# Two layers planned in one list, the second layer's first chunk prepared within the first layer

## Chip, cores and metric

The kernel runs on one core of a Trainium2 chip. The metric is the device time of one execution in microseconds. A core has five engines with queues of their own, each worked through in order: PE (matrix products and transposes), DVE (vector work and the scans), ACT (activations and copies), POOL (elementwise work) and SP, which here issues the DMAs. Engines wait for one another by semaphores. Work that waits at the head of a queue holds everything behind it.

## What is computed

A network of two layers over two batches of 2048 rows of 256 values, all in float32. Each layer is a state-space block followed by a feed-forward part. Layer 0 has a scan over 256 channels with 16 states and an expert part that sends each row through chosen small networks; layer 1 is a bidirectional Mamba (a forward and a backward pass over each batch, 512 channels, 16 states) with a small feed-forward network, and a second feed-forward whose weights go through a butterfly transform. Cut to what matters:

```python
def _selective_scan(u, dt, A, Bm, Cm, Dp):
    h0 = jnp.zeros((u.shape[0], D_INNER, D_STATE), u.dtype)
    def step(h, inp):
        u_t, dt_t, B_t, C_t = inp
        dA = jnp.exp(dt_t[:, :, None] * A)
        h = dA * h + (dt_t * u_t)[:, :, None] * B_t[:, None, :]
        y = jnp.einsum('bds,bs->bd', h, C_t)
        return (h, y)
    ...

def _mamba(x, Win, convw, convb, Wx, Wdt, bdt, Alog, Dp, Wout):
    xz = x @ Win
    xi, z = jnp.split(xz, 2, axis=-1)
    xi = jax.nn.silu(_causal_dwconv(xi, convw, convb))
    xdbc = xi @ Wx
    ...
    dt = jax.nn.softplus(dt_in @ Wdt + bdt)
    A = -jnp.exp(Alog)
    y = _selective_scan(xi, dt, A, Bm, Cm, Dp)
    return y * jax.nn.silu(z) @ Wout
```

Layer 1 normalises the sum that layer 0 leaves (x1, kept in DRAM as x1d, one tensor for each batch) and feeds it to `_mamba`.

## The kernel before

**A planner sets the order.** Every piece of work is an `op`: an engine, an estimated duration, a Python function that emits the instructions, a key (when it is due), the ops it depends on, and the rings of buffers that it takes (`takes`). `Plan.order` walks the ops as a list scheduler: on each engine it picks, among those that could start at once, the one with the smallest key; an op that takes a buffer may not run further ahead of the oldest unfinished scan than `ahead` key units. The order it returns is the order on PE, DVE, ACT and POOL. DMAs on SP are placed by the framework. `spread` gives a group of ops keys in a given interval.

**Layer 0** (`layer0`) has 8 chunks of 512 rows, 4 for each batch, 32 key units each. A chunk has 16 pairs of scans. A pair goes through ACT (two decays, L1140), PE (two sources, L1164), DVE (two scans, L1172), POOL (the last column kept, L1187, and the product with cb, L1191), PE (the collecting matmul, L1195). Its cb and G come by DMA (L1148, L1152) into rings of three. Beside the scans run: the prologues of both batches; `prepare` of the next chunk; the experts, eight groups `experts(b, ec)` due one every 27 key units from key 12 (L664 to L840: gather, first and second matmul, store to interd, relay, back-projection, added to xacc); two butterflies (`butterfly_ops`) which make the weights wup and wdn for layer 1 and store them. The end of a chunk is `finish` (the output matmul L1226, added to xacc at L1233); when all ten sums of a quarter of a batch are in, xacc is stored to x1d (L651).

**Layer 1** (`layer1`) has 16 chunks of 512 rows (forward and backward, two batches), 64 key units each, 64 scans each (L1935, with sources L1922, decays L1904, products L1954, collecting L1966, fills of the source rows on ACT L1846 and POOL L1848). Before a chunk's scans comes its preparation. For the first chunk this is `prologue(0, 0)`: two halves of 256 rows, each loaded from x1d (L1401), moments (L1375, L1376), the root on POOL (L59, L60), normalised (L81), turned on PE (L1414), copied (L1421); the second half is loaded only when the first is copied. Then `prepare(0)`: the projection (L1606), a copy (L1613), the halo (L1618 to L1621), the convolution's taps on DVE (L1631), SiLU (L1689), the projection to dt, B and C (L1700, L1706, L1730, L1741, L1754), softplus (L1770), dt times u (L1784), turned and copied (L1793, L1799). In later chunks the same work runs beside the scans of the chunk before. The second prologue, `prologue(0, 1)`, and the loads of layer 1's weights (`load_in`, `load_z`, `load_out`, `load_ff`) are due before or at the start of the first chunk. `load_ff` loads eight small rows (L1516 to L1529), wup, wdn and two feed-forward weights (L1545 to L1555), and sums the bias rows on POOL (L1537 to L1540).

**Between the layers** stands a wall. Each layer has a plan of its own, and each opens its memory pools and its eight PSUM banks on entry and closes them on leaving. Layer 1's pools take the place of layer 0's, and its list begins when layer 0's has been emitted in full:

```python
    layer0(tc, c, a, x1d, wupd, wdnd, bupd)
    layer1(tc, c, a, x1d, wupd, wdnd, bupd, out)
```

Of the kernel before, what the change touches and what calls it, by code (L numbers as in the profile page):

```python
# [10 lines left out]
F32 = mybir.dt.float32  # L11
# [8 lines left out]
B = 2  # L20
# [79 lines left out]
EARLY0, GATE0, PREP0, FIN0, PRO0, EXP0, BFLY0 = -2, (10, 15), (8,30), (4, 12), ((-1, 8), (4, 14)), (12, 27), ((8, 110), (114, 200))  # L100

SLACK = 0.15

# [251 lines left out]
def layer0(tc, c, a, x1d, wupd, wdnd, bupd):  # L355
    nc = c.nc
    with ExitStack() as ctx:
        c.banks(ctx, sums=4, work=2)
        wp = ctx.enter_context(tc.tile_pool(name="w0", bufs=1))
        fp = ctx.enter_context(tc.tile_pool(name="ffn0", bufs=1))  # L360
        ap = ctx.enter_context(tc.tile_pool(name="attn0", bufs=1))
        sp = ctx.enter_context(tc.tile_pool(name="scan0", bufs=1))
        bf = ctx.enter_context(tc.tile_pool(name="bfly", bufs=1))

        xnd = [c.dram.tile([L, D], F32, name=f"xnd{b}") for b in range(B)]
        xnTd = [c.dram.tile([P, 2, L], F32, name=f"xnTd0{b}") for b in range(B)]
        interd = [
            [c.dram.tile([P, 16, D], F32, name=f"interd{b}{ec}") for ec in range(4)] for b in range(B)
        ]


        rings = {
            "pp": 2, "ab": 2, "yacc": 4, "xp": 1, "lt": 1, "xq": 2, "selT": 1, "pb": 2, "PT": 4,
            "f1": 1, "f2": 1, "inner": 1, "stage": 2, "relay": 2, "xacc": 4, "xnT": 3, "zs": 1,
            "cv": 2, "uw": 1, "par": 1, "dt": 3, "dw": 3, "lk": 1, "a": RING0, "cb": CB0, "G": 3,
            "bfy": 1, "bft": 1, "bf8": 2,
        }
        pl = Plan(rings, AHEAD0)
        op, inline = pl.op, pl.inline

        def rows4(ref, q):

            return ref.rearrange("(n p) d -> p n d", p=P)[:, 4 * q : 4 * q + 4, :]

        W, M = {}, {}
# [3 lines left out]
        def weights():  # L389
            def first():  # L390
                W["cw"] = wp.tile([P, 2, 4], F32, name="cw")
                nc.sync.dma_start(W["cw"], a["conv0"].rearrange("(k p) c -> p k c", p=P))
                W["wpar"] = wp.tile([P, 2, 112], F32, name="wpar")
                nc.sync.dma_start(W["wpar"], a["wpT"].rearrange("(k p) e -> p k e", p=P))
                W["wdt"] = wp.tile([64, 512], F32, name="wdt")
                nc.sync.dma_start(W["wdt"], a["wdtT"])
                W["bdt"] = wp.tile([P, 4], F32, name="bdt")
                nc.sync.dma_start(W["bdt"], a["dt0"])

            def scans():  # L400
                W["A"] = wp.tile([P, 4, NS], F32, name="A")
                nc.sync.dma_start(W["A"], a["A0"])
                W["As"] = wp.tile([P, 4, 8], F32, name="As")
                nc.sync.dma_start(W["As"], a["A0s"])
                W["D0"] = wp.tile([64, 4], F32, name="D0")
                nc.sync.dma_start(W["D0"], a["D0"])

            def other():
                W["ctrl"] = wp.tile([P, 2, 64], F32, name="ctrl")
                nc.sync.dma_start(W["ctrl"], a["ctrl"].rearrange("(k p) e -> p k e", p=P))  # L410
                W["wz"] = wp.tile([P, 2, D], F32, name="wz")
                nc.sync.dma_start(W["wz"], a["wzT"].rearrange("(k p) e -> p k e", p=P))
                W["wo"] = wp.tile([P, 2, D], F32, name="wo")
                nc.sync.dma_start(W["wo"], a["woT"].rearrange("(k p) d -> p k d", p=P))
                W["fbias"] = wp.tile([P, 32], F32, name="fbias")
                nc.sync.dma_start(W["fbias"], a["fbias"])

            def exps():
                nc.scalar.activation(W["As"], W["As"], AF.Exp)
                nc.scalar.activation(W["A"], W["A"], AF.Exp)  # L420

            def factors():
                A = W["A"]
                nc.vector.tensor_scalar(W["As"], W["As"], -1.0, None, ALU.mult)

                small = wp.tile([P, 4, NS], F32, name="small")
                nc.vector.tensor_scalar(small, A, 1e-5, None, ALU.is_lt)
                large = wp.tile([P, 4, NS], F32, name="large")
                nc.vector.tensor_scalar(large, small, -1.0, 1.0, ALU.mult, ALU.add)
                c1 = wp.tile([P, 4, NS], F32, name="c1")  # L430
                nc.vector.tensor_scalar(c1, A, -1.0, 1e-10, ALU.mult, ALU.add)
                nc.vector.tensor_mul(c1, c1, large)
                nc.vector.tensor_sub(c1, c1, small)
                nc.vector.reciprocal(c1, c1)
                nc.vector.tensor_mul(c1, c1, large)

                cf = W["cf"] = wp.tile([P, 4, NS], F32, name="cf")
                nc.vector.tensor_copy(cf[0:64], c1[0:64])
                nc.vector.tensor_copy(cf[64:P], small[64:P])
                fold = W["fold"] = wp.tile([P, 64], F32, name="fold")  # L440
                nc.vector.tensor_add(fold, c.ident[:, 0:64], c.ident[:, 64:P])
                W["Gd"] = c.dram.tile([P, 4, 8, P], F32, name="Gd")

            def sources(h):

                if h == 0:
                    W["G"] = fp.tile([P, 4, NS, 64], F32, tag="selT", name="G")
                G = W["G"]
                nc.vector.tensor_mul(
                    G[:, h],  # L450
                    W["fold"].unsqueeze(1).broadcast_to([P, NS, 64]),
                    W["cf"][:, h].unsqueeze(2).broadcast_to([P, NS, 64]),
                )

            def store(h):
                nc.sync.dma_start(
                    W["Gd"][:, h].rearrange("p m e -> p (m e)"),
                    W["G"][:, h].rearrange("p n e -> p (n e)"),
                )

            def lacks():

                nc.vector.tensor_scalar(W["cf"][0:64], W["cf"][0:64], -1.0, None, ALU.mult)

            def turn():
                W["ps"] = c.pp()
                for h in range(4):
                    nc.tensor.transpose(
                        W["ps"][0:16, h * P : (h + 1) * P], W["cf"][:, h], c.ident
                    )  # L470

            def turned():
                W["cl"] = wp.tile([112, 2, P], F32, name="cl")
                v = W["ps"][0:16].rearrange("p (e h c) -> p e h c", h=2, c=P)
                for h in range(2):
                    nc.vector.tensor_copy(W["cl"][64 + 32 * h : 80 + 32 * h], v[:, :, h])

            def masks():
                tie_i = W["tie_i"] = wp.tile([64, 16], I32, name="tie_i")
                nc.gpsimd.iota(tie_i, pattern=[[1, 16]], base=0, channel_multiplier=0)  # L480

                block = W["block"] = wp.tile([P, 8, 16], F32, name="block")
                nc.gpsimd.memset(block, 1.0)
                nc.gpsimd.affine_select(
                    out=block, in_=block, compare_op=ALU.is_ge, fill=0.0, base=0,
                    pattern=[[-16, 8], [0, 16]], channel_multiplier=1,
                )
                nc.gpsimd.affine_select(
                    out=block, in_=block, compare_op=ALU.is_ge, fill=0.0, base=15,
                    pattern=[[16, 8], [0, 16]], channel_multiplier=-1,  # L490
                )

            def ties():
                tie = W["tie"] = wp.tile([64, 16], F32, name="tie")
                nc.vector.tensor_copy(tie, W["tie_i"])
                nc.vector.tensor_scalar(tie, tie, 1e-6 / 15.0, None, ALU.mult)

            M["first"] = op(SP, 0.3, first, key=-40)
            s = M["scans"] = op(SP, 0.3, scans, key=-39)
            M["w"] = op(SP, 0.4, other, key=-36)  # L500
            e = op(ACT, 0.45, exps, s, key=-39, table="exp")
            f = op(DVE, 2.0, factors, e, key=-38)
            M["As"] = f
            M["G"] = []
            for h in range(4):
# [3 lines left out]
                if h == 0:  # L509
                    g0 = g  # L510
# [8 lines left out]

        def prologue(b, q, k0, k1, keep=None):
            S = {}
            n0 = len(pl.ops)

# [1917 lines left out]
```

## Time and profile before

| | us |
|---|---|
| median of 3 executions | 2895.32 (2892.51 to 2903.18) |
| the profiled execution, whole | 2900.49 |
| its span, first to last instruction | 2898.4 |
| busy PE, DVE, ACT, POOL | 2634.8 (91%), 2366.5 (82%), 2153.3 (74%), 2246.7 (78%) |
| layer 0: first scan starts, last scan ends | 51.5, 884.0 |
| layer 0's chunks 0 to 7, first scan to last | 97.6, 107.5, 113.7, 114.7, 102.3, 95.1, 112.8, 79.5 |
| layer 1: first scan starts, last scan ends | 966.6, 2838.5 |
| layer 1's chunks 0 to 3 | 100.5, 112.7, 110.9, 111.5 |

A profile is of one execution, so lengths within it belong to 2898.4, not to the median. The busy share of PE is modelled: its matmuls overlap. A line such as L1172 is the line of the program that made the instruction. The chain of work that ended last has PE for 38% of the span, DVE for 14% and POOL for 10%; its heaviest single lines (PE L1922 10%, PE L1966 8%, DVE L1935 7%, POOL L1954 7%) are layer 1's scans and their neighbours.

### The profile page before, as it was taken

Reading aid. Unit: us, or ns where it says so; the run is one execution under the profiler, and the core shown is the slowest. Engines: PE = TensorE matmul, PEld = TensorE weight load, DVE = VectorE, ACT = ScalarE, POOL = GpSimd, SP = SyncE. Lnnn points to the kernel's source line nnn. Section 1 sums busy time; section 2 is a strip of 40 time slices with the busy share of each in tenths; the row PEclk is TensorE's granted clock in tenths of the full one; section 3 lists DMA queues with packets and bytes.
Section 4 is the critical chain, followed back from the end, with each engine's and each line's share of the span. In section 5 each row is a group of like instructions: output and inputs, shape, how many; then the busy total and the mean of one; then the engine's idle time right before and its main releaser. Section 6 shows DMA issues by size and latency. Waiting matters only on the chain.

```text
span 2898.4 us, 43538 instructions
## 1 busy us (share of the span) xinstructions
PE 2634.8 (91%) x15268; PEld 1878.3 (65%) x15268; DVE 2366.5 (82%) x2508; ACT 2153.3 (74%) x3301; POOL 2246.7 (78%) x2149
## 2 busy tenths in 40 slices
PE   6888998999994899999999899999999999999997
PEld 2334543444442577777777777778787788787875
DVE  5967776676664689989889999898898988989894
ACT  4645755657641998988988888788889898887871
POOL 2867447754442699989899999898998998988894
PEclk7999999999997999999999999999999999999998
DMA  6576467755554121321131222222212212121211
GB/s 222 171 211 186 142 186 226 244 167 171 161 159 159 51 82 46 98 71 59 56 97 47 88 85 67 91 81 70 70 52 82 63 59 84 55 67 56 66 59 55
DMA packets 256203, 308.92 MB, mean 107 GB/s; under 512 B 25264, under 2 KB 190256, under 8 KB 254064
## 3 DMA queue, kind: packets, MB, share of 16 engines
q1 hardware_dynamic: 255984, 306.13, 34.0%
q8 instruction: 121, 1.98, 0.3%
q14 instruction: 98, 0.80, 0.1%
HBM read 246.55 MB, written 59.51 MB: 106 GB/s over the span
## 4 chain that ended last, share of the span: by engine, by line
PE 38%; DVE 14%; POOL 10%; issue 4%; ACT 2%; DMA 1%; SPq 0%; POOLq 0%; DVEq 0%; ACTq 0%
PE ab L1922 10%; PE yacc L1966 8%; DVE a L1935 7%; POOL a L1954 7%; PE pp L2150 3%; PE pp L2036 3%; PE pp L1606 3%; PE pp L2107 2%; PE pp L1577 2%; PE pp L2218 2%; POOL bT L1848 2%; DVE xn L81 2%; DVE pp L1631 1%; PE pp L1700 1%; PE pp L2246 1%
## 5 line engine op out<-in xcount | busy, mean ns | idle before, releaser
L1954 POOL TENSOR_TENSOR a<-a,cb 128x1024 f32<-128x1024 f32 x512 | 1216.7, 2376 | 29.7 <-POOL hc L1948 0.2
L1935 DVE TENSOR_TENSOR_SCAN a<-a,hc,ab 128x512 f32<-128x512 f32 x768 | 943.5, 1266 | 84.2 <-PE ab L1922 63.5
L1904 ACT ACTIVATE a<-dt,A 128x512 f32<-128x512 f32 x1024 | 677.4, 716 | 46.4 <-PE yacc L1966 30.3
L1922 PE MATMUL ab<-ident,bT 128*128 128x128 f32 x4096 | 626.5, 277 | 56.8 <-DVE a L1935 48.5
L1922 PEld LDWEIGHTS ab<-ident,bT 128*128 128x128 f32 x4096 | 486.7, 142 | 240.3 <-DVE a L1935 138.5
L1966 PE MATMUL yacc<-ident,a 128*128 128x128 f32 x4096 | 562.5, 275 | 22.3 <-POOL a L1954 22.1
L1966 PEld LDWEIGHTS yacc<-ident,a 128*128 128x128 f32 x4096 | 470.9, 141 | 63.5 <-POOL a L1954 35.2
L1846 ACT ACTIVATE bT<-dtuT,BT 128x512 f32<-128x512 f32 x640 | 423.8, 714 | 26.5 <-PE ab L1922 26.5
L1935 DVE TENSOR_TENSOR_SCAN a<-a,ab 128x512 f32<-128x512 f32 x256 | 299.4, 1206 | 37.0 <-PE ab L1922 30.3
L1172 DVE TENSOR_TENSOR_SCAN a<-ab,hn,a 128x512 f32<-128x512 f32 x192 | 242.2, 1275 | 102.8 <-PE ab L1164 97.9
L1191 POOL TENSOR_TENSOR a<-a,cb 128x1024 f32<-128x1024 f32 x128 | 307.6, 2403 | 10.4 <-POOL hn L1187 0.3
L1187 POOL COPY hn<-a 128x2 f32<-128x2 f32 x128 | 50.2, 393 | 322.5 <-DVE a L1172 302.9
L1164 PE MATMUL ab<-dw,Gm 128*128 128x512 f32 x512 | 275.9, 636 | 15.0 <-DVE a L1172 8.4
L1848 POOL TENSOR_SCALAR bT<-dtuT,BT 128x512 f32<-128x512 f32 x384 | 273.3, 716 | 8.0 <-ACT dtuT L1799 3.3
L1140 ACT ACTIVATE a<-dt,As 128x512 f32<-128x512 f32 x256 | 173.4, 715 | 132.5 <-PE yacc L1195 61.2
L1164 PEld LDWEIGHTS ab<-dw,Gm 128*128 128x128 f32 x512 | 85.5, 194 | 136.0 <-issue 65.9
L1948 POOL COPY hc<-a 128x2 f32<-128x2 f32 x512 | 107.7, 210 | 82.8 <-DVE a L1935 80.1
L1195 PE MATMUL yacc<-a,fold 128*64 128x512 f32 x512 | 137.7, 616 | 8.5 <-POOL a L1191 8.5
L1606 PE MATMUL pp<-xnT,winx 128*128 128x512 f32 x256 | 128.6, 607 | 5.7 <-DVE zu L1631 4.8
L2036 PE MATMUL pp<-wout,ygT 128*128 128x256 f32 x512 | 130.7, 381 | 2.7 <-DVE zu L1631 2.5
L1577 PE MATMUL pp<-winz,xnT 128*128 128x512 f32 x256 | 126.7, 602 | 4.2 <-DVE zu L1631 4.2
L2107 PE MATMUL pp<-xnT,wup 128*128 128x256 f32 x512 | 122.9, 385 | 3.7 <-ACT gff L2116 1.0
(200 smaller groups left out, 4128.1 us busy)
## 6 DMA issues: line engine op xcount, KB each, us to landing
cb<-bcd SPq DMA_DIRECT2D x256, 256.0 KB, 3.2
cb<-cd SPq DMA_DIRECT2D x256, 128.0 KB, 3.1
Gm<-Gd SPq DMA_DIRECT2D x128, 128.0 KB, 3.2
xnq<-xnd SPq DMA_DIRECT2D x32, 512.0 KB, 5.4
f<-in_f_dram SPq DMA_DIRECT2D x32, 512.0 KB, 4.9
interd<-stage SPq DMA_DIRECT2D x64, 256.0 KB, 4.5
relay<-interd SPq DMA_DIRECT2D x64, 256.0 KB, 3.4
xnTd<-xnT SPq DMA_DIRECT2D x16, 512.0 KB, 4.2
```

The source lines that it names most:

```text
L1164: nc.tensor.matmul(R["x", h], R["G"][:, h, :], ck.dw[e][:, h, :], start=True, stop=True)
L1172: nc.vector.tensor_tensor_scan(v, R["x", h], v, 0.0 if ck.first else pv.hn[:, k, h : h + 1], ALU.add, ALU.mult,)
L1191: nc.gpsimd.tensor_mul(v, v, R["cb"].unsqueeze(1).broadcast_to([P, 2, T]))
L1606: nc.tensor.matmul(S["ps"], w["winx"][:, k, e * P : (e + 1) * P], ck.xnT[:, k, :], start=(k == 0), stop=(k == 1),)
L1846: nc.scalar.activation(t, ck.dtuT[:, q, :], AF.Copy, scale=v)
L1848: nc.gpsimd.tensor_scalar(t, ck.dtuT[:, q, :], v, 1.0, ALU.mult, ALU.mult)
L1904: nc.scalar.activation(R["a"][:, h], ck.dt[:, e0 + h], AF.Exp, scale=w["A"][:, e0 + h, n : n + 1],)
L1922: nc.tensor.transpose(R["b", h][:, q * P : (q + 1) * P], ck.bT[n, q][:, e * P : (e + 1) * P], c.ident,)
L1935: nc.vector.tensor_tensor_scan(v[:, step], v[:, step], b[:, step], 0.0 if ck.first else pv.hn[:, e, n : n + 1], ALU.mult, ALU.add,)
L1954: nc.gpsimd.tensor_mul(v, v, ck.cb[n].unsqueeze(1).broadcast_to([P, 2, T]))
L1966: nc.tensor.matmul(ck.y[e][:, tb * P : (tb + 1) * P], v[:, tb * P : (tb + 1) * P], c.ident, start=False, stop=(n == NS - 1), is_transpose= ...
L2036: nc.tensor.matmul(S["ps"][:, n * D : (n + 1) * D], ck.ygT[:, e, q * P : (q + 1) * P], ck.w["wout"][:, e, :], start=(e == 0), stop=(e == 3),)
```

## The change

Both layers become one list of ops in one `Plan`, ordered in one go, with one set of PSUM banks. Layer 1's keys are rescaled to follow layer 0's (`STEPS0 + PACE * key`, so 64 units of layer 1 are 35.2 of the plan), and its first prologue is due at -75 to -58 of its own units, which is 214.75 to 224.1 of the plan; layer 0's last chunk has the keys 224 to 256. The planner's `ahead` is layer 0's 4 for both (layer 1 had 7 in its own units, 4 is 7.3 of them).

Pools are opened and closed from within the list. They are of a class `Late` that opens a pool when told, on the left or right side of memory, with waits for reused memory set tile by tile. On the right side stand layer 0's pools of the experts and butterflies, replaced (op `sw1`) when their last op is done by layer 1's pools for the direction's weights, the preparation and the normalised rows. On the left stand layer 0's weights, preparation and scans, replaced (op `sw2`) when all of layer 0 is done by layer 1's shared weights, scans and feed-forward. Both ops emit no instruction; layer 1's ops depend on the one whose memory they use. So its preparation may run once the experts are through, its scans, fills and the loads of `load_ff` only after layer 0's end.

To free the right side sooner, the experts of batch 1 are due from key 127 at one every 20 units (from 120, every 27). xacc moves to a left pool. `finish` of the last chunk is due at 256 to 258 rather than 260 to 268, the loads of batch 1's xacc at 140 rather than 172. Rings that both layers had under one name get a name for each. The indentation of both layers changes, which makes every line of them part of the full diff; its core, without that:

```diff
+FIRST, SECOND, STEPS0, PACE = (-75, -58), (-60, 0), 256, 0.55
+class Late:
+    def __init__(self, tc, name, bufs=1, side="left"):
+        self.args = dict(name=name, bufs=bufs, side=side, reuse_waits="tile")
+        self.tc = tc
+    def open(self):
+        self.cm = self.tc.tile_pool(**self.args)
+        self.pool = self.cm.__enter__()
+    def close(self):
+        self.cm.__exit__(None, None, None)
+    def tile(self, *args, **kw):
+        return self.pool.tile(*args, **kw)
...
-            fetch_sums(b, q, (K * (NT + 1) + 8) * b + 4)
+            fetch_sums(b, q, (K * NT + 8) * b + 4)
...
-            finish(i, K * (i + 1) + FIN0[0], K * (i + 1) + FIN0[1])
+        finish(i, *((K * (i + 1) + k for k in FIN0) if i + 1 < len(steps) else (K * (i + 1), K * (i + 1) + 2)))
...
         for p in range(2 * 4):
-            at = EXP0[0] + EXP0[1] * p
-            experts(p // 4, p % 4, at, at + EXP0[1], at + 2 * EXP0[1])
+        at, n = (EXP0[0] + EXP0[1] * p, EXP0[1]) if p < 4 else (EXP1[0] + EXP1[1] * (p - 4), EXP1[1])
+        experts(p // 4, p % 4, at, at + n, at + 2 * n)
...
-            ld = op(SP, 0.1, load, *copies, takes=("xnT", "x1t") if h == 0 else ("x1t",))
+            ld = op(SP, 0.1, load, sw1, x1_stores[b, k], *copies, takes=("xnT", "x1t") if h == 0 else ("x1t",))
...
-        r = op(SP, 0.6, rows)
-        x = op(SP, 0.2, extra, takes=("xn", "xn"))
+        r = op(SP, 0.6, rows, sw2)
+        x = op(SP, 0.2, extra, sw2, takes=("xn", "xn"))
...
-        pl.spread(n0, -140, -120)
+    pl.spread(n0, *FIRST)
...
+    for o in pl.ops[start:]:
+        o.key = STEPS0 + PACE * o.key
+    return pl.ops[start:]
...
-    layer0(tc, c, a, x1d, wupd, wdnd, bupd)
-    layer1(tc, c, a, x1d, wupd, wdnd, bupd, out)
+    c.banks(ctx, sums=4, work=2)
...
+    pl = Plan(rings, AHEAD0)
+    left0 = [Late(tc, n) for n in ("w0", "attn0", "scan0")]
+    right0 = [Late(tc, n, side="right") for n in ("ffn0", "bfly")]
+    right1 = [Late(tc, n, k, "right") for n, k in (("wdir", 1), ("mamba", 2), ("row1", 1))]
+    left1 = [Late(tc, n, k) for n, k in (("w1", 1), ("scan1", 4), ("tmp1", 1))]
...
+    r, x1_stores, ops0 = layer0(tc, c, a, pl, pools, x1d, wupd, wdnd, bupd)
+    last = max(o.key for o in r)
+    sw1 = pl.op(SP, 0.0, lambda: swap(right0, right1), *r, key=last)
+    sw2 = pl.op(DVE, 0.0, lambda: swap(left0, left1), *ops0, key=STEPS0)
+    layer1(tc, c, a, pl, pools, x1d, wupd, wdnd, bupd, out, x1_stores, sw1, sw2)
+    swap([], left0 + right0)
+    with tc.manual_schedule(engines={nc.tensor.engine, nc.scalar.engine, nc.vector.engine, nc.gpsimd.engine}):
+        for o in pl.order():
+            o.f()
+    swap(left1, [])
+    swap(right1, [])
```

## Prediction

> **What bounds the kernel now.** I read first the slices of the page, to see where no engine is full. One slice is 72.5 us; the thirteenth (869 to 942 us) stands out on every engine.
>
> ```profile
> PE   6888998999994899999999899999999999999997
> DVE  5967776676664689989889999898898988989894
> ACT  4645755657641998988988888788889898887871
> POOL 2867447754442699989899999898998998988894
> PEclk7999999999997999999999999999999999999998
> ```
>
> Then busy time by stage, with stages cut at the scans (L1172 in layer 0, L1935 in layer 1): layer 0's chunks 5, 6 and 7, the stretch between the layers, layer 1's chunk 0. Columns: stretch, length, then busy us of PE, weight load, DVE, ACT, POOL, the granted clock, DMA share, GB/s.
>
> ```profile
> 595.10:690.50 95.40, 92.87 (x396) 43.47 (x394) 73.35 (x85) 66.54 (x109) 49.88 (x38) 0.98 0.52 161
> 690.50:804.60 114.10, 106.36 (x508) 57.58 (x508) 70.69 (x73) 69.20 (x108) 47.73 (x38) 1.00 0.52 164
> 804.60:884.00 79.40, 73.26 (x266) 31.16 (x264) 50.31 (x49) 27.50 (x43) 39.41 (x31) 0.98 0.48 146
> 884.00:966.60 82.60, 36.52 (x125) 20.10 (x124) 20.66 (x43) 30.16 (x45) 14.11 (x28) 0.75 0.43 140
> 966.60:1070.70 104.10, 92.95 (x626) 73.78 (x625) 92.85 (x92) 98.58 (x150) 97.74 (x100) 1.00 0.18 56
> ```
>
> Layer 0 is paced by PE (92 to 97% busy in these chunks, DVE 62 to 77%); layer 1 has PE, DVE, ACT and POOL all near 90%. Between them 82.6 us pass without a scan, and no engine is half full. The timeline there (start, us, engine, line; in brackets the idle time before and what ended it) shows one chain:
>
> ```profile
> 881.59 2.46 DVE L1172 TENSOR_TENSOR_SCAN a<-ab,hn,a 128x512 f32<-128x512 f32 x2 [0.75 <-PE ab L1164]
> 884.38 2.34 POOL L1191 TENSOR_TENSOR a<-a,cb 128x1024 f32<-128x1024 f32 x1
> 886.77 1.08 PE L1195 MATMUL yacc<-a,fold 128*64 128x512 f32 x4 [2.56 <-POOL a L1191]
> 888.66 3.29 PE L1226 MATMUL pp<-wo,zs 128*128 128x256 f32 x14 [0.19 <-DVE zs L1207]
> 893.19 0.38 SPq L651 DMA_DIRECT2D x1d<-xacc  x1
> 907.37 1.88 DVE L81 TENSOR_SCALAR xn<-x1t,mv,rs 128x256 f32<-128x256 f32 x4 [13.59 <-POOL obias L1539]
> 922.10 0.43 DVE L1375 BATCH_NORM_STATS2 bs<-x1t 128x6 f32<-128x256 f32 x1 [12.85 <-DMA x1t<-x1d]
> 942.64 1.91 ACT L1689 ACTIVATE zu<-zu 128x2048 f32<-128x2048 f32 x1
> 966.63 10.24 DVE L1935 TENSOR_TENSOR_SCAN a<-a,ab 128x512 f32<-128x512 f32 x9 [5.99 <-PE ab L1922]
> ```
>
> The last scan of layer 0 ends at 884.05, its output projection at 891.95, the last store is issued at 893.19. All after that is layer 1's first chunk made ready: two halves loaded and normalised (to 925), projection and convolution (to 942), SiLU, parameters, softplus, transposes (to 963), first scan at 966.63. None of it needs that last store: it reads batch 0, stored long before.
>
> **The change, part by part.** The built programs hold the same instructions but for one activation table load more (131 for 130; 1.28 us in this trace, on ACT, 27.5 us busy of 79.4 in chunk 7: nothing). So only places move. I counted each engine's list between scans, before and after. Up to layer 0's chunk 4 and from layer 1's chunk 2 the counts agree but for about 2 us; costs fall in four stages. For PE, whose matmuls overlap, I price an instruction by the time it adds to the union of PE's busy time.
>
> *Chunks 5 and 6: the experts of batch 1 come sooner.* Chunk 5 gains 16 back-projections (L833, 0.54), 16 gathers (0.24), 16 first (0.14) and 8 second (0.28) expert matmuls and 16 transposes (0.13), less two L1105: +17.7 us of PE. Chunk 6 loses 9.3. PE is nearly full there, nothing hides it: +8.4. Bounds: 0, since DVE has 65 us idle in the two, and 17.
>
> *Chunk 7: the preparation moves in.* PE gains 16 transposes L1414 (2.8), 8 L1606 (7.2), 4 L1700 (3.6), 4 L1730 (2.2), 4 L1754 (0.5), 16 L1793 (1.9), 18.2 us, and loses 8.4 of expert work: +9.8. DVE gains 8 L1375, 8 L1376, 12 L1631 (0.75 each), 3 L1784 and 8 L81, less three others: +22.8 us, against 29.1 idle. Beside POOL's products L81 is dear: of its 160 in the trace the 77 that overlap a product take 1397 ns on average, the other 83 take 582; at the mean of 974 that I used, eight lack 8 x 0.42 = 3.4 us. POOL gains 6.6 us (40 idle), SP some two dozen issues of 0.4 to 0.6 us among loads of cb that wait on POOL for 29.1 us of this chunk. If all hides in idle time, 0; if DVE's share is simply added, 22.8 + 3.4 = 26; PE alone at its 94% share, 9.8/0.94 = 10.4. I take 15.6, a third of the way from PE's 10.4 to DVE's 26, since PE is the fuller engine. Layer 0 grows by 8.4 + 15.6 = 24, bounds 0 and 43.
>
> The Trainium skill, SBUF — State Buffer, section "Who interferes with whom", says that a two-port DVE operation and a GpSimd one hold their shared port exclusively, the loser waiting out the whole instruction; by that rule the products could as well be held, 8 x 0.58 = 4.7 us on POOL, which has 40 idle, so 3.4 us less and 2849; but the trace shows the wait on DVE (1397 against 582 ns) and the product unmoved (2.37 us beside a scan, 2.39 beside L81), so the sum keeps the 3.4.
>
> *The gap.* In the new order PE has, after the last output matmul, 16 transposes that add the skip term (L1881, two groups of 1.04) and then the first source (4 transposes, 0.66). From the last scan: 891.95 - 884.05 + 2.1 + 0.7 = 10.7 us to the first scan of layer 1, instead of 82.6. Fills on POOL (4 of 0.7 after the last product) are ready by then. If the new pools' tiles must wait for the last store to land (893.19 + 2.92), then fills and source: 896.1 + 2.7 + 0.7 - 884.05 = 15.5. That is the upper bound; 10 the lower.
>
> *Start of layer 1.* The loads that need the old pools' memory now stand behind the last store on SP: eight small rows (0.45 each), the first cb, four weight tensors of 3.1 MB, then the next cb. First cb: 893.19 + 0.38 + 3.6, landing 3.5 us later, about 900.8; POOL's sums of the bias rows (L1537 to L1540) stand before the first product too. So the first product comes 6.0 us after the first scan (894.8), against 2.7 now (969.29). 3.1 MB at the 400 GB/s seen at 910 to 920 take 8 us, so the second cb lands near 909 for a product due at 908. I take +4; with 3.6 us net more of PE in chunks 0 and 1, mostly beside this, +5. Bounds 0 and 16: the weights took 9.0 to 10.7 us to land before. A queue of nine ring buffers lets 18 scans run on meanwhile, but POOL is 94% busy in this chunk and doesn't win the time back.
>
> Sum: -82.6 + 10.7 + 24 + 5 = -42.9. The profiled execution took 2900.5 us (span 2898.4, 2.1 around it), 5.2 over the median; 2895.3 - 42.9 = **2852 us**.
>
> **Rivals.**
> *Layer 0 absorbs it all* (chance 0.16). For: DVE, ACT and POOL are idle for 29 us and more in chunk 7, and a busy PE is only modelled. Against: PE's 97% in chunk 5. Layer 0 +3, start +3: -82.6 + 10.7 + 6 = -66, 2829 us. The Trainium skill speaks for this one (Perfetto Trace Analysis, "Identifying the Most-Contended Engine": matmul busy time misjudges PE, weight-load busy time is the measure, and that is 46 to 50% of chunks 5 and 6 here).
>
> *Layer 1 starves at its start* (0.15): cb and bias rows late behind the weights, first products stall. For: the 1.5 to 2 times longer landings in today's hole. Gap 15.5, start +14: -82.6 + 15.5 + 24 + 14 = -29, 2866 us.
>
> *It slides out* (0.07): the preparation stands in the order early but its loads come late on SP (the second half of x1t is loaded only after the first is turned), so convolution and after (927 to 967, 40 us, with 5 to get there) still follow the last scan, and layer 0 grows a little less: -82.6 + 45 + 20 + 5 = -13, 2882 us. This is where the change would not do what it says. Against: in the built order PE's and DVE's whole part of it stands ahead of layer 0's last scan.
>
> *Lock-step, slower* (0.07): the preparation is some 25 dependent steps across five in-order queues, and each holds the scans behind it for one product (2.36 us): 59 us in chunk 7, with 8.4 and 10.4 of PE 78, so -82.6 + 10.7 + 78 + 5 = +11, 2906 us. It decides once layer 0 grows by more than 67 us. For: scans in layer 0 wait for PE in 18 of 32 cases in chunk 7. Against: the planner puts scans between the steps.
>
> **How the numbers follow.** Forecast 0.55, with its own range 2838 to 2868 (the bounds of chunk 7 and the start, not all at once). About 0.5%, 14.5 us, is what a measurement of this kernel can tell from no change. Faster: 0.55 + 0.16 + 0.15 = 0.86; within: 0.07; slower: 0.07. The range goes from 2826 (all absorbed) to 2888 (slid out), leaving out lock-step and tails.
>
> **What would show it.** Chunk 5 near 113 us, chunk 6 near 105, chunk 7 near 95; first L1935 scan some 11 us after the last L1172; granted clock near 1.0 in place of 0.75 around it; first L1954 product some 6 us after that scan; chunks from layer 1's second on unchanged within 1%. It would be wrong if chunk 7 passes 130 us, if the gap stays above 40, or if later chunks change, which the equal order excludes.

## The result, and the profile after

The changed kernel takes 2871.63 us, the median of 4 executions (2868.0 to 2875.17); the kernel before, run beside it, 2899.06 (2892.51 to 2903.18). The ratio is 0.9907 with a 95% interval of 0.9881 to 0.9933: 27.4 us, where 42.9 were forecast. The time lies outside the forecast's own range (2838 to 2868) and inside the outer one (2826 to 2888). The profiled execution took 2875.17 us, its span 2873.5 (24.9 less than the 2898.4 before).

The slices of the changed kernel, 71.8 us each; the hole of the thirteenth is gone:

```profile
PE   6889988998998799999999899999999999999997
DVE  5967776677467789989989999998898988989884
ACT  4636755567457698898998888888889898887871
POOL 2867346753255899989899999898899998989894
PEclk7999998999999999999999999999999999999998
```

The timeline where the hole was (start, us, engine, line; in brackets the idle time before):

```profile
919.27 1.28 DVE L1182 TENSOR_TENSOR_SCAN a<-ab,hn,a 128x512 f32<-128x512 f32 x1
...
925.19 3.29 PE L1236 MATMUL pp<-wo,zs 128*128 128x256 f32 x14 [0.19 <-DVE zs L1217]
...
928.31 1.91 PE L1882 MATMUL yacc<-ident,a 128*128 128x128 f32 x16
...
930.06 1.04 PE L1923 MATMUL ab<-ident,bT 128*128 128x128 f32 x8
930.77 2.33 DVE L1936 TENSOR_TENSOR_SCAN a<-a,ab 128x512 f32<-128x512 f32 x2 [1.57 <-ACT a L1905]
```

The last scan of layer 0 ends at 920.55 and the first of layer 1 (L1936 now, L1935 before) starts at 930.77. What stands between is what the forecast named: the output matmuls, the 16 skip transposes, the first source. Busy time by stage, layer 0's chunks 5, 6, 7, the gap, layer 1's chunk 0 (stretch, length, busy us of PE, weight load, DVE, ACT, POOL, granted clock, DMA share, GB/s):

```profile
599.00:716.20 117.20, 109.44 (x513) 58.01 (x512) 89.88 (x97) 77.77 (x126) 52.58 (x40) 0.97 0.51 161
716.20:827.10 110.90, 102.62 (x459) 49.66 (x458) 62.27 (x62) 66.16 (x104) 44.54 (x35) 0.98 0.53 164
827.10:920.60 93.50, 85.27 (x260) 34.10 (x258) 69.70 (x86) 46.52 (x65) 46.84 (x50) 0.95 0.51 154
920.60:930.80 10.20, 8.40 (x47) 5.90 (x48) 2.10 (x4) 9.96 (x17) 5.26 (x7) 1.00 0.22 73
930.80:1056.70 125.90, 103.23 (x658) 81.50 (x657) 93.78 (x95) 96.21 (x147) 105.19 (x106) 0.92 0.27 86
```

| stage, us | before | after | difference | forecast |
|---|---|---|---|---|
| layer 0, chunks 3 and 4 | 223.1 | 227.9 | +4.8 | 0 |
| chunk 5 | 95.4 | 117.2 | +21.8 | +17.7 |
| chunk 6 | 114.1 | 110.9 | -3.2 | -9.3 |
| chunk 7 | 79.5 | 93.5 | +14.0 | +15.6 |
| between the layers | 82.6 | 10.2 | -72.4 | -71.9 |
| layer 1, chunks 0 and 1 | 216.8 | 236.1 | +19.3 | +5 |
| layer 1, chunks 2 to 15 | 1655.1 | 1645.8 | -9.3 | 0 |

The hole closed as forecast. Of its 72 us, layer 0 took 36.7 back (24 forecast; chunks 1 and 2, not in the table, changed by -0.7) and the start of layer 1 took 19.3 (5 forecast). The -9.3 at the end was in no term of the forecast. It sits mostly in chunks 7 and 14 of layer 1 (3.7 us each). A kernel whose layer 1 is the unchanged one (the first experiment) has 1650.2 there, with chunk 14 as fast as here, and the changed order ran there between 1642.8 and 1652.9 us in the profiles below; so it need not be the change's, and some of the profiled gain is chance.

The start of layer 1. First the longest waits in that chunk (who waited for whom: us in all, times, longest), then POOL's timeline, then SP's:

```profile
DVE a L1936 <- PE ab L1923: 21.4, 10, 14.6
...
PE pp L2108 <- DMA wup<-wupd: 12.2, 1, 12.2
...
POOL fwnb L1538 <- DMA fwnb<-in_fwn_b_dram: 8.6, 1, 8.6
```

```profile
923.34 2.71 POOL L1849 TENSOR_SCALAR bT<-dtuT,BT 128x512 f32<-128x512 f32 x4
934.69 0.87 POOL L1538 TENSOR_SCALAR fwnb<-fwnb 128x256 f32<-128x256 f32 x1 [8.65 <-DMA fwnb<-in_fwn_b_dram]
...
941.97 2.34 POOL L1955 TENSOR_TENSOR a<-a,cb 128x1024 f32<-128x1024 f32 x1 [0.23 <-DMA cb<-bcd]
951.47 0.19 POOL L1949 COPY hc<-a 128x2 f32<-128x2 f32 x1 [7.15 <-DVE a L1936]
```

```profile
929.23 0.37 SPq L661 DMA_DIRECT2D x1d<-xacc  x1
929.65 0.50 SPq L1517 DMA_DIRECT2D fwnw<-in_fwn_w_dram  x1
...
934.12 0.36 SPq L1837 DMA_DIRECT2D cb<-bcd  x1
934.68 2.20 SPq L1546 DMA_DIRECT2D wup<-wupd  x2
```

Two heads of queues block here. On PE the first up projection of the feed-forward (L2108) stands in line and waits 12.2 us for wup, whose loads were issued only at 934.68; every source behind it is late, so the scans wait too (one wait of 14.6 us). On POOL the sums of the bias rows (L1538 to L1541) stand ahead of the first product, which comes 11.2 us after the first scan (6.0 forecast, 2.7 before).

### The profile page after: what moved, and what is told of

Read it like the earlier page. It is cut to its first block, busy times and chain, and to the rows that moved or that the text cites. A ratio compares the mean times of both kernels' runs of the same rounds, so it can differ in the third digit from the quotient of the medians.

```text
span 2873.5 us, 43499 instructions
## 1 busy us (share of the span) xinstructions
PE 2639.9 (92%) x15268; PEld 1877.2 (65%) x15268; DVE 2378.0 (83%) x2508; ACT 2153.4 (75%) x3302; POOL 2245.8 (78%) x2149
## 4 chain that ended last, share of the span: by engine, by line
PE 53%; POOL 16%; DVE 14%; issue 7%; DMA 5%; ACT 4%; SPq 1%; POOLq 0%; DVEq 0%; ACTq 0%
PE ab L1923 10%; POOL a L1955 8%; PE yacc L1967 8%; DVE a L1936 6%; PE ab L1174 5%; PE pp L2151 3%; PE pp L2037 3%; PE pp L1607 3%; POOL a L1201 3%; PE pp L2108 3%; PE yacc L1205 2%; PE pp L1578 2%; PE pp L2219 2%; POOL bT L1849 2%; DMA interd<-stage 2%
## 5 line engine op out<-in xcount | busy, mean ns | idle before, releaser
L1936 DVE TENSOR_TENSOR_SCAN a<-a,hc,ab 128x512 f32<-128x512 f32 x768 | 941.6, 1264 | 78.2 <-PE ab L1923 60.2
L1967 PE MATMUL yacc<-ident,a 128*128 128x128 f32 x4096 | 563.7, 275 | 18.9 <-POOL a L1955 18.6
L1936 DVE TENSOR_TENSOR_SCAN a<-a,ab 128x512 f32<-128x512 f32 x256 | 299.1, 1206 | 48.8 <-PE ab L1923 37.2
L1201 POOL TENSOR_TENSOR a<-a,cb 128x1024 f32<-128x1024 f32 x128 | 306.1, 2391 | 10.4 <-POOL hn L1197 0.3
L1174 PEld LDWEIGHTS ab<-dw,Gm 128*128 128x128 f32 x512 | 86.6, 197 | 143.6 <-issue 64.9
L1949 POOL COPY hc<-a 128x2 f32<-128x2 f32 x512 | 108.5, 212 | 82.6 <-DVE a L1936 80.1
L2108 PE MATMUL pp<-xnT,wup 128*128 128x256 f32 x512 | 124.6, 388 | 14.8 <-DMA wup<-wupd 12.2
```

Of the source, the lines that this page charges most:

```text
L1174: nc.tensor.matmul(R["x", h], R["G"][:, h, :], ck.dw[e][:, h, :], start=True, stop=True)
L1201: nc.gpsimd.tensor_mul(v, v, R["cb"].unsqueeze(1).broadcast_to([P, 2, T]))
L1936: nc.vector.tensor_tensor_scan(v[:, step], v[:, step], b[:, step], 0.0 if ck.first else pv.hn[:, e, n : n + 1], ALU.mult, ALU.add,)
L1967: nc.tensor.matmul(ck.y[e][:, tb * P : (tb + 1) * P], v[:, tb * P : (tb + 1) * P], c.ident, start=False, stop=(n == NS - 1), is_transpose= ...
```

## The experiments

Stages below are cut as above; "chunks 1 to 7" are layer 0's, 735.0 us before and 771.7 in the changed kernel. A profile is of one execution. Six profiles have layer 0 with the same work in the same order (the changed kernel, experiments 2 to 5 and the second profile in 5): chunks 1 to 7 took 764.9 to 774.9 us in them. A difference of some 10 us in layer 0 between two single profiles can therefore be chance.

**1. The earlier experts alone, in the kernel before.**

```diff
-            at = EXP0[0] + EXP0[1] * p
-            experts(p // 4, p % 4, at, at + EXP0[1], at + 2 * EXP0[1])
+            at, n = (EXP0[0] + EXP0[1] * p, EXP0[1]) if p < 4 else (127 + 20 * (p - 4), 20)
+            experts(p // 4, p % 4, at, at + n, at + 2 * n)
```

> The kernel before with one part of the change alone: batch 1's experts at the planner's places of the change (from key 127, 20 apart, where they stood at 120, 27 apart); two lists, two sets of pools, the hole between the layers untouched. Theory (the growth of layer 0's chunks 3 to 6 is the experts' alone): chunk 5 goes from 95 to 113-118 us, chunk 6 from 114 to 105-111, chunk 7 from 79.5 to 69-74 as 8 us of expert work leave it, the hole stays at 82-83 and layer 1 does not move; the total is 2 to 12 us above the kernel before. Rival (the growth comes of the preparation and the shared rings that it passes through): chunk 5 stays below 102, chunk 7 near 79, the total is within 3 us of the kernel before. Open beforehand: whether the 10 us more in chunk 3 and 5 less in chunk 4 belong to the experts; if they do, both show here.

Measured: 2913.25 us beside 2905.27, ratio 1.0034 (1.0019 to 1.0050): 8.0 us more, within the 2 to 12 expected. Chunk 3 is 6.5 longer, chunk 4 3.5 shorter, chunk 5 9.8 and chunk 6 7.2 longer, chunk 7 3.4 shorter: +15.2 in chunks 1 to 7. The hole is 83.7, chunks 0 and 1 of layer 1 216.8. So the earlier experts cost by themselves, and the shift between chunks 3 and 4 shows with them alone; but the growth stands in chunks 5 and 6 alike, not as expected in 5 alone, and chunk 7 gave back 3.4 us where 5 to 10 were expected.

**2. to 4. The two queue heads at the start of layer 1**, each alone and both, in the changed kernel.

```diff
-        network(i, steps[i - 1].o_out if i else [], *(NET if i else (2, 62)))
+        network(i, steps[i - 1].o_out if i else [steps[0].o_scan[6]], *(NET if i else (2, 62)))
```

> The changed kernel with the up projection of layer 1's first network held back behind that chunk's 14th scan; nothing else. Theory (in the changed kernel TensorE stands 12.2 us at that projection's first matmul, whose weights land late, and everything behind it in TensorE's queue is late): the wait is gone, chunk 0 of layer 1 goes from 125.9 to 113-118 us, chunk 1 stays near 110, the total falls by 8 to 13 us. Rival (the chunk is paced by GpSimd, whose first product comes 11.2 us after the first scan because of the bias rows and the late cb): the chunk stays above 121 and the total falls by less than 4 us.

```diff
         scans(i)
+        if i == 0:
+            FW["o_rows"].deps.append(steps[0].o_scan[6])
```

> The changed kernel with GpSimd's sums of the bias rows (four instructions at the head of layer 1) held back behind the first chunk's 14th scan; the up projection stays where it is. Theory (TensorE's wait for the up weights decides): the first product starts earlier, 4 to 9 us after the first scan where it was 11.2, but TensorE's wait of about 12 us stays, and chunk 0 stays at 121-126 us, the total falls by less than 4 us. Rival (GpSimd decides): chunk 0 falls to 115-119 us and the total by 6 to 10.

> Both of the edits above on the changed kernel: the up projection and the bias sums behind the 14th scan. Theory (the 19 us that layer 1's first two chunks grew by are these two queue heads and nothing else): chunks 0 and 1 together go from 236 to 217-221 us, the total to 2853-2858, 14 to 18 us below the changed kernel. Rival (the late loads themselves, cb behind 3 MB of weights, set the start, whatever stands at the queue heads): chunks 0 and 1 stay above 227, and the gain is below 9 us.

| kernel | median, us | ratio (interval) | first product after first scan | PE's wait for wup | chunks 0 + 1 |
|---|---|---|---|---|---|
| changed | 2871.63 | 0.9907 (0.9881 to 0.9933) | 11.2 | 12.2 | 236.1 |
| up projection later | 2867.09 | 0.9874 (0.9854 to 0.9894) | 11.0 | none | 230.1 |
| bias sums later | 2875.46 | 0.9912 (0.9882 to 0.9941) | 11.2 | 12.1 | 237.4 |
| both later | 2876.09 | 0.9903 (0.9883 to 0.9923) | 11.5 | none | 232.6 |

The first row has a measurement of the kernel before of its own (2899.06), the other three share one (2905.27), so the ratios are to be compared. The up projection alone gave 6 us of the 19: chunk 0 fell to 118.9, just outside the 113 to 118 expected. The median fell by 4.5 us, or by 10.8 if each kernel is taken against its own kernel before (8 to 13 expected); not all of that is the edit's, for layer 0, in the same order, took 764.9 us in this profile and 771.8 in the changed kernel's. With the bias sums alone moved, chunk 0 stayed at 125.7 as the theory had it, but the first product came no earlier, which it had not. With both, the start was no better than with the first: the theory that these two queue heads are all of it fell, and chunks 0 and 1 stayed above 227 as its rival had it. POOL's timeline of the kernel with both edits says why:

```profile
926.39 2.70 POOL L1849 TENSOR_SCALAR bT<-dtuT,BT 128x512 f32<-128x512 f32 x4
936.22 0.19 POOL L1949 COPY hc<-a 128x2 f32<-128x2 f32 x1 [7.13 <-DVE a L1936]
945.35 2.34 POOL L1955 TENSOR_TENSOR a<-a,cb 128x1024 f32<-128x1024 f32 x1 [8.95 <-DMA cb<-bcd]
```

With the bias sums away, the product itself waits 8.95 us, for cb. In the changed kernel the bias sums hid this: cb, issued on SP at 934.12 behind the eight rows, landed only at 941.97 (the 0.23 us that the product still waits there are for it), and the sums happened to end just before.

**5. cb first.** The rows and weights follow the first three loads of cb; bias sums and up projection behind the 22nd scan.

```diff
         FW["o_rows"], FW["o_up"], FW["o_dn"] = s, u, [dn]
+        FW["loads"] = [r, x, u, dn, FW["o_ff"]]
...
-        ck.o_hn = ck.o_scan
+        ck.o_hn, ck.o_cbs = ck.o_scan, cbs
...
         scans(i)
+        if i == 0:
+            FW["o_rows"].deps.append(steps[0].o_scan[10])
+            for o in FW["loads"]:
+                o.deps.append(steps[0].o_cbs[2])
...
-        network(i, steps[i - 1].o_out if i else [], *(NET if i else (2, 62)))
+        network(i, steps[i - 1].o_out if i else [steps[0].o_scan[10]], *(NET if i else (2, 62)))
```

> The changed kernel with layer 1's first three loads of cb put ahead of the eight small rows and the four weight tensors in SyncE's queue, and the bias sums and the first network's up projection held back behind the 22nd scan. Theory (three things stand in series at the start of layer 1: cb behind rows and weights, the bias sums at the head of GpSimd's queue, the up projection at the head of TensorE's; each alone, and the two last together, gained little because the next one takes over): the first product starts 3-5 us after the first scan (11.2 in the changed kernel), no wait above 5 us is left in that chunk on TensorE, chunks 0 and 1 together go from 236 to 217-222 us, the total falls by 12-18 us to 2854-2860. Rival (the fourth and later cb behind 3 MB of weights, or GpSimd's own work, keep the chunk long): chunks 0 and 1 stay above 226 and the gain is below 9 us.

Measured: 2858.5 us beside 2900.87, ratio 0.9855 (0.9836 to 0.9873), its interval below that of the changed kernel. SP's and POOL's timeline of it (lines are up to one further down):

```profile
924.71 0.37 SPq L661 DMA_DIRECT2D x1d<-xacc  x1
925.18 1.93 SPq L1838 DMA_DIRECT2D cb<-bcd  x3
927.16 0.43 SPq L1517 DMA_DIRECT2D fwnw<-in_fwn_w_dram  x1
```

```profile
931.14 2.35 POOL L1956 TENSOR_TENSOR a<-a,cb 128x1024 f32<-128x1024 f32 x1 [2.31 <-DMA cb<-bcd]
933.43 0.19 POOL L1950 COPY hc<-a 128x2 f32<-128x2 f32 x1
933.69 2.36 POOL L1956 TENSOR_TENSOR a<-a,cb 128x1024 f32<-128x1024 f32 x1
```

The first product starts 4.9 us after the first scan (926.24), the second follows at once, the longest wait of PE in the chunk is 1.7 us, and chunks 0 and 1 take 224.9 us: 11.2 less than in the changed kernel, not quite down to the 217 to 222 expected (the rival had them above 226). Of the 8.1 us still above the kernel before, PE has 3.9 more to do there (205.5 us busy for 201.6), work that the hole used to hold; the rest was not followed further. The same kernel once more, measured beside the two of experiment 8:

> A second look at the kernel with cb first, on this chip, beside the two above. Expected: as before, layer 0's chunks 1 to 7 at 765-775 us, the gap at 10-11, chunks 0 and 1 of layer 1 at 224-226, the span at 2852-2864.

It gave 769.6 us for chunks 1 to 7, 10.2 for the gap, 225.0 for chunks 0 and 1 and a span of 2861.2.

**6. No overlap: one list, but layer 1's pools opened after all of layer 0.**

```diff
-    sw1 = pl.op(SP, 0.0, lambda: swap(right0, right1), *r, key=last)
-    sw2 = pl.op(DVE, 0.0, lambda: swap(left0, left1), *ops0, key=STEPS0)
+    sw1 = pl.op(SP, 0.0, lambda: swap(right0, right1), *ops0, key=last)
+    sw2 = pl.op(DVE, 0.0, lambda: swap(left0, left1), *ops0, sw1, key=STEPS0)
```

> The changed kernel (one list, one set of banks, experts early), but with the pools of layer 1 opened only when all of layer 0's operations are done, so that no part of layer 1's preparation can stand beside layer 0. Theory (what pays is the overlap alone, and the early experts are its price): the hole is back at 76-86 us, layer 0's chunks 1 to 7 grow as with the experts alone, by about 15 us, chunk 7 is near 76, and the total is 2903-2918, above the kernel before. Rival (one list and one set of banks pay by themselves, for instance through a shorter start of layer 1): the total stays at or below 2890.

Measured: 2897.02 us beside 2900.87, ratio 0.9986 (0.9973 to 1.0000). The hole is back at 75.6 us and chunks 1 to 7 take 742.3 (7.3 over the kernel before, not 15), chunk 7 66.8, chunks 0 and 1 of layer 1 216.0. The total lies between the theory's 2903 to 2918 and the rival's 2890, so both missed. Most of the gain is the overlap's: without it the ratio goes from 0.9907 to 0.9986. One list, one set of banks and the early experts come together to -3.9 us, with an interval that ends at no change. As the early experts alone cost 8.0 us in the first experiment, the list and the banks would be worth some 12 us if the two simply add (an estimate; the hole is 8.1 and layer 0 7.9 us shorter here than there); no run has them without the early experts and without the overlap. The starting cost in layer 1 is the overlap's too, for without it the start is as short as before.

**7. Where the experts stand.** In the changed kernel back at their old places:

```diff
-... EXP0, EXP1, BFLY0 = ... (12, 27), (127, 20), ...
+... EXP0, EXP1, BFLY0 = ... (12, 27), (120, 27), ...
```

> The changed kernel with the experts of batch 1 at the places they have in the kernel before (from key 120, 27 apart); everything else as changed. Theory (the experts had to be hurried because layer 1's right-hand pools wait for their memory): the built order has the normalising, convolution and everything behind it after the last scan of layer 0, so layer 0 is back to within 5 us of the kernel before, but the stretch between the layers is 60-83 us, and the total is 2880-2905. Rival (the preparation finds its way in anyway and the hurry only cost): layer 0 grows by 15-20, the gap stays below 25, the total falls below 2865.

Measured: 2883.25 us beside 2900.87, ratio 0.9937 (0.9921 to 0.9953). The gap is 58.8 and chunks 1 to 7 take 750.5. Most of the preparation did slide behind the last scan, as the theory has it (58.8 is just below its 60 to 83, the total within its range), but layer 0 was 15.5 us longer, not within 5: as many matmuls of PE as before (2914 recorded in those chunks), only in another order. Two more places, both with cb first, (124, 23) and (120, 18):

> The kernel of the run before it (cb first) with the experts of batch 1 at a middle place: from key 124, 23 apart (changed: 127 and 20; before: 120 and 27). The built order still has all of the preparation but one product of step size and input ahead of the last scan of layer 0. Theory (the growth of chunks 3 to 6 is the crowding of the experts): layer 0's chunks 1 to 7 grow by 22-32 us over the kernel before instead of 37, the gap is 10-18, the total lies 3-10 us below the run before it. Rival (the growth is the preparation's work and does not depend on the spacing): layer 0 as with 127 and 20 within 3 us, total equal or above it by what the gap loses.

> The kernel with cb first, and the experts of batch 1 earlier and closer (from key 120, 18 apart; changed: 127 and 20): no expert work is left in layer 0's chunk 7, which holds the preparation alone, and chunk 4 has more of it. Theory (layer 0 is TensorE's time over a fixed share of about 91.5%, wherever the work stands): chunk 7 falls to 80-87 us, chunks 4 to 6 take it back, chunks 1 to 7 stay at 765-776, the total stays within 6 us of the kernel with cb first (2858 to 2863). Rival (chunk 7 is a crowd of experts and preparation, and parting them saves): chunks 1 to 7 fall below 760 and the total below 2852.

With (124, 23): 2874.15 us beside 2900.87, ratio 0.9908 (0.9890 to 0.9927), chunks 1 to 7 772.8, gap 13.7: wider spacing saved nothing in layer 0, as the rival had it; but the total is 15.7 us above experiment 5's, not by the 3.5 that the gap lost, and what the rest is was not followed. With (120, 18): 2872.11 beside 2902.52, ratio 0.9890 (0.9860 to 0.9920). Its chunk 4 and chunk 7 (columns as above):

```profile
485.60:623.10 137.50, 120.35 (x520) 61.54 (x516) 76.52 (x76) 66.64 (x101) 84.87 (x56) 0.90 0.73 231
...
857.30:930.00 72.70, 71.10 (x218) 26.40 (x216) 59.78 (x62) 42.12 (x60) 43.68 (x44) 1.00 0.38 122
```

Chunk 7, with the preparation and no expert in it, falls to 72.7 us and runs at 98% of PE; chunk 4 takes 29 us more than in the kernel before, and chunks 1 to 7 come to 782.5. Parting the two saves nothing. PE's 707.6 us over 91.5% would be 773, so some 9 us came on top, most likely from the crowd in chunk 4; both expectations missed, the rival by more.

**8. Which engine prices the moved work.** The first half of each input projection of layer 1's first chunk computed seven times; or its normalisations three times.

```diff
-                nc.tensor.matmul(
-                    S["ps"], w["winx"][:, k, e * P : (e + 1) * P], ck.xnT[:, k, :],
-                    start=(k == 0), stop=(k == 1),
-                )
+                for j in range(6 if k == 0 and ck is steps[0] else 0, -1, -1):
+                    nc.tensor.matmul(
+                        S["ps"], w["winx"][:, k, e * P : (e + 1) * P], ck.xnT[:, k, :],
+                        start=(k == 0), stop=(k == 1 or j > 0),
+                    )
```

> The changed kernel with more of TensorE's work in the moved preparation: the first half of each of the four input projections of layer 1's first chunk (128x512, about 0.6 us each) is computed seven times instead of once, 24 instructions and some 14 us of TensorE time in layer 0's chunk 7; the order of everything else is the same. Theory (layer 0 is paced by TensorE at a fixed share of about 91.5%, which it has had in every kernel so far, so what is moved in costs its TensorE time over that share): chunk 7 goes from 88-94 us to 103-110, and chunks 1 to 7 from 765-775 to 780-790. Rival (the preparation costs by VectorE, or by its chain of steps, and TensorE has room): chunk 7 stays below 98.

```diff
-                c.normalize(S["n"], S["v"], S["mv"], S["rs"], 2)
+                for _ in range(3 if b == 0 and k < 2 else 1):
+                    c.normalize(S["n"], S["v"], S["mv"], S["rs"], 2)
```

> The changed kernel with more of VectorE's work in the moved preparation: each normalisation of layer 1's first two tiles is computed three times instead of once, 16 more instructions of 0.6 to 1.4 us, some 15 us of VectorE time in layer 0's chunk 7; the order of everything else is the same. Theory (TensorE sets the pace, VectorE has 24 us idle in that chunk): chunk 7 grows by less than 5 us, to at most 98. Rival (VectorE's time beside the scans counts, as the forecast had it by a third): chunk 7 grows by 8 to 15 us, to 98-108.

Chunk 7 with more of PE's work:

```profile
830.20:940.70 110.50, 103.58 (x308) 42.23 (x307) 70.24 (x86) 46.44 (x65) 46.63 (x50) 0.98 0.43 131
```

and with more of DVE's:

```profile
825.00:920.60 95.60, 86.57 (x260) 33.06 (x258) 76.63 (x102) 46.66 (x65) 46.84 (x50) 0.95 0.50 151
```

One execution each, 2900.33 us in all with more of PE's work and 2870.61 with more of DVE's, beside 2899.15 for the kernel before. PE is busy 18.3 us longer than in the changed kernel (some 14 were meant) and the chunk 17.0 us longer (93.5 to 110.5, just above the 103 to 110 expected; chunks 1 to 7 took 791.3, just above 780 to 790). DVE is busy 6.9 us longer (the repeated instructions took 0.43 us each, so this is half the load that was meant) and the chunk is 2.2 us longer, at 95.7. In the six profiles of the unchanged order this chunk took between 88.6 and 93.8 us. Against these, PE's added time is paid in full or nearly so. For DVE the length alone settles less: the chunk grew by 1.9 to 7.0 us for 6.9. What speaks against a price of DVE's is PE's idle time in the chunk, 9.1 us where the six have 6.5 to 8.3: little of the added work made PE wait. The rest is PE's own busy time, 86.6 us, which varies from 81.5 to 85.5 among the six.

## Why the prediction came out as it did

*What bounds the kernel, and the gap: right.* The chain between the layers did not need the last store, and 82.6 us became 10.2, where 10.7 was worked out from the same three pieces. The granted clock there went from 0.75 to 1.00.

*Chunk 7, +15.6 forecast, +14.0 measured: near by the sum, but not by the reason, and in part by luck.* I put it a third of the way from PE's 10.4 to DVE's 26. Experiment 8 shows PE's time counts. PE's busy time grew by 12.0 in the chunk (73.3 to 85.3), not by the 9.8 priced, and at the 91% that PE was busy this makes 13.2. Over the six profiles of this order the chunk grew by 9.2 to 14.3 us, 11.5 in the mean, nearer to the 10.4 that PE alone would have made than to 15.6. L81 beside POOL's products was priced too dear: its eight instructions took 384 to 2448 ns, 662 in the mean with a median of 411, where 974 was used and 3.4 us added.

*"Chunks 5 and 6: the experts of batch 1 come sooner", +8.4, bounds 0 to 17: mis-sized; it measured 18.6, and chunks 3 and 4, priced at nothing, 4.8.* Chunk 5 held: PE +16.6 against the 17.7 priced, and 5 us more of idle PE, above all for relay loads (PE waited 6.2 us for them in this chunk, 1.2 before). Chunk 6 gave back 3.7 us of PE instead of 9.3. And an order seems to have a price of its own: with the same work in chunks 1 to 7 (2912 to 2914 recorded matmuls) the kernel before and experiments 1, 6 and 7 took 735.0, 750.2, 742.3 and 750.5 us, with PE busy for 674.7, 684.2, 679.5 and 684.5 at a granted clock of 0.97, 0.96, 0.97 and 0.96. The two longest have the lower clock. Of one profile each, and with the 10 us by which one order varies, only the 15 us of experiments 1 and 7 stand out, and experiment 1's 8.0 us by the median; whether the order lowers the clock through its waits was not tested. What did not move is PE's share of the time; the two lines are chunks 1 to 7 of the kernel before and of the changed one:

```profile
149.00:884.00 735.00, 674.70 (x2914) 327.33 (x2910) 510.18 (x537) 426.22 (x665) 415.07 (x312) 0.97 0.60 184
```

```profile
148.80:920.60 771.80, 705.67 (x2978) 338.29 (x2974) 543.19 (x576) 450.83 (x699) 417.85 (x330) 0.96 0.60 183
```

91.8% and 91.4%. It was 90.4 to 91.8% in every kernel of this study whose whole stretch was read, with PE busy from 675 to 725 us. 31.0 us more of PE at that share are 34 us; 36.8 came. My sum had 18.2 us of PE for the three chunks. Priced by instruction counts it missed what the clock adds: in chunk 3, with 441 recorded matmuls where there were 461 (20 had moved on to chunk 4), PE was busy 4.6 us longer, at a granted clock of 0.92 where it was 0.99. Over the eight profiles that share this order up to there, chunk 3 took 119.3 us with PE busy 104.0 at a clock of 0.97, and up to 124.9 with 107.4 at 0.92.

*"Start of layer 1", +5, bounds 0 to 16: the worst miss; 19.3 came.* The mechanism was there as the rival "Layer 1 starves at its start", which the forecast priced at 14 with a gap of 15.5; the gap did not come, the starving did. The step that failed is "3.6 us net more of PE in chunks 0 and 1, mostly beside this": among that work was L2108, which stands in PE's queue after the first two sources (eight transposes) and needs wup, the very load that I had landing late. It held PE for 12.2 us. The first product came 11.2 us after the first scan and not 6.0, because cb took 7.8 us from issue to landing (934.12 to 941.97), not the 3.5 that I used, and was issued 4.9 us behind the last store's issue, not 4.0. Experiment 5 shows what all of it was worth, late cb, bias sums and L2108 together: 11.2 us back, of which L2108 alone gave 6.0. Its total, 42.4 us below its own kernel before, is close to the forecast's 42.9 by chance: layer 0 still grew by 33.9 where 24 were forecast, and layer 1's later chunks were again 8.7 us shorter, where nothing was.

*Rivals.* "Layer 0 absorbs it all" fell: PE's time is paid in full or nearly so. The rule of the Trainium skill that spoke for it (Perfetto Trace Analysis, "Identifying the Most-Contended Engine") tells TensorE's headroom by weight-load busy time and the share of peak arithmetic, not by matmul busy time. In experiment 8 the chunk had weight loads for 36% of its time before the addition (34.1 of 93.5) and still grew by 17.0 us for 18.3 us more of matmul busy time, so in this kernel the measurement decides for the busy time. By the total, the rival "Layer 1 starves at its start" (-29) came nearer to the measured -27.4 than the forecast did, but its parts did not come: it had the gap at 15.5 and layer 0 at +24. "It slides out" was not the case here; experiment 7 produced it in part by giving the experts their old places (gap 58.8). "Lock-step" did not occur: layer 0 grew by 37, not by 67.

*Marks.* Gap, clock and chunk 7 as said; chunk 5 at 117 (113 said), chunk 6 at 111 (105), the first product 11.2 us after the first scan (6). Of the later chunks of layer 1, chunks 1, 4, 7, 8, 14 and 15 moved by 1.1 to 2.9%, not within 1%; between the kernel before and experiment 1, whose layer 1 is the same, chunk 14 moved by 3.7 us as well, so the mark was too narrow for a single profile.

## What to carry to other kernels

A hole between two stages is worth its length less what its work costs where it goes: take the busy time of the engine that paces the destination, over the share at which it runs there, and allow some per cent more for the disturbed order (here the measured growth of layer 0 was half as large again as the sum). When the next stage starts earlier, look in each in-order queue for the first instruction that needs a late load (here wup on PE, bias rows on POOL, cb behind rows on SP): they stand in series, so removing one moves the wait to the next, and loading in order of first use (experiment 5) took most of them at once. A table of waits can hide an earlier load's lateness behind a later one: cb showed as 0.23 us of wait until the bias sums ahead of it were moved, then as 8.95.

## What the runs showed of the hardware

PE's wait has an after-cost through the clock. In chunk 3 of layer 0 the granted clock was 0.92 after the change (0.99 before, by the windows), with PE waiting 5.4 and 4.6 us for ACT and 2.6 us for DVE there. The source matmuls of that chunk in the kernel before, then after (duration in ns, minimum, median, maximum):

```profile
L1164 PE MATMUL ab<-dw,Gm x64: 592/592/697, 373.9 to 486.1; 128*128 128x512 f32 x64
```

```profile
L1174 PE MATMUL ab<-dw,Gm x65: 592/592/1222, 373.0 to 495.3; 128*128 128x512 f32 x65
```

Some take 1222 ns, 2.06 times the median; they stand in the 7 us behind the 4.6 us wait. The granted clock was 0.50 right behind each of the three waits (429.1 to 433.7, 448.6 to 451.8 and 488.8 to 496.0 us). The Trainium skill (TensorE: Matmul & The Clock Gate, "What's actually happening") has the clock at half or full speed only, the half after an idle window of about 3.4 us. The factor agrees with it; the length of the wait agrees only roughly, since the clock also halved behind the wait of 2.6 us, and in the kernel before it stayed at 1.00 behind one of 2.8 us (446.6 to 450.5). In layer 1's first chunk the granted clock was 0.92 with the 12.2 us wait, and 1.00 in both profiles of the kernel with cb first.

The normalisations on DVE (L81) took 575 ns on average over the 24 of experiment 8, in a chunk in which POOL's products fill 37.8 of 95.6 us: 20 of them fell beside no product and took 405 on average, and two took 2446 and 2451. Which of the two engines starts first matters: of the 77 that overlap a product in the kernel before, the 45 that started during one took 1883 ns on average, the 32 that had started before it 714; the product took 2377 and 2409.
